# A transformer block on one core: the last key block read in two parts, low parts ahead of reads on GpSimd's queue, normed rows in a tile of their own, and token loads ahead of sums

## The chip, the core and the metric

The kernel runs on one core of a Trainium2 chip. The time is the device time of one execution in microseconds, as a median of several executions. Engines: TensorE (PE, with its weight loads as PEld), VectorE (DVE), ScalarE (ACT), GpSimd (POOL) and SyncE (SP). SP, ACT and POOL issue DMAs, each in the order of its own queue; POOL computes and issues in one and the same order. Engines wait for one another on semaphores.

## The reference

A conditioned transformer block in float32, for x of shape (2, 2048, 576), with 16 heads of 36 and an MLP of 2304:

```
mod = silu(c) @ w_ada + b_ada            # six vectors per batch: shifts, scales, gates
xn  = layernorm(x) * (1 + sc_msa) + sh_msa
q, k, v = split(xn @ w_qkv + b_qkv);  q = layernorm_head(q);  k = layernorm_head(k)
o   = softmax(q k^T / 6) v               # per batch and head
x   = x + g_msa * (o @ w_proj + b_proj)
xn2 = layernorm(x) * (1 + sc_mlp) + sh_mlp
x   = x + g_mlp * (gelu(xn2 @ w1 + b1) @ w2 + b2)
```

## The kernel before

Two bodies are built and one is chosen at run time; for these inputs it is `block_of_small`. Its stages are, for each batch b: inputs (`inputs`), attention (`attend`), output projection (`outputs`); then the MLP for both batches. PE runs in the order in which the program is written throughout. In `inputs`, DVE, SP and POOL run in written order too; in `attend`, DVE, POOL and ACT; in `outputs` and the MLP, DVE alone. The rest is put in order by the scheduler when the program is built.

**Inputs.** 16 token tiles of 128 rows. A tile is loaded (`tile_loaded`), normed, transposed in squares of 32 on DVE, written to DRAM (`squares_turned`, line 1003, four DMAs on POOL) and read back with features on partitions (`turned_loaded`, lines 1011 and 1013, three DMAs). ACT applies scale and shift (line 1020). The last 64 of the 576 features are kept as a rounded high part (line 388) and a low part, which is the difference of an exact copy (`tail`, line 389) and the high part; POOL makes that difference (line 390). A product of a tile (`product`) has, for each half of the columns, eight records of line 1100 and then two of line 1102, of which the second reads the low part. The loop over t calls `begun(t)` (load of tile t+4, read of tile t+2, both on POOL), `modulated_ahead(t)` (ACT's lines and POOL's low part for tile t+1), the products, `turned_ahead(t)` (norm, transposition and writes of tile t+3), and the head norms. In the first batch the first three tiles come another way (transposed on PE), beside the loading and centring of the weights. There `bias_made` centres the bias on DVE and has POOL write it to DRAM, and `bias_spread` has POOL read it back to all partitions.

Q and K are put in DRAM with features as rows (`qk`): `by_feature(t)` transposes on DVE (line 1078) and issues four writes (line 1080), on SP except for the K half of tile 15, which goes on POOL. `take_k_block` reads back the 72 K rows of the first head pair for a range of tiles (lines 812 and 814, four DMAs on SP) and returns a function that applies gain and bias on DVE: line 847 on `km` (32 of 36 features of a head), and lines 847, 856, 857 on `ke` (the remaining four, in high and low parts). The ranges are tiles 0-3, 4-7, 8-11, 12-15. The first three run inside `inputs`; the function of the last is returned as `left`.

**Attention.** For each head pair p (8), query block qb (4 of 512) and key group g (4), one step: `scores` (line 1225: 24 matmul records into eight PSUM banks, then eight exponentials on ACT, line 1229), then `values` of the step before (line 1238: 16 records into one bank), then DVE copies or adds that bank to `ot` (lines 1286, 1288), then the functions due in `later[0]` run. Group g reads columns 256g to 256g+255 of `km` and `ke`, where partitions 0-63 hold keys of tiles 0-7 and partitions 64-127 those of tiles 8-15: group 2 needs tiles 4, 5, 12, 13 and group 3 needs tiles 6, 7, 14, 15. At the first step `left` is put in front of `later[1]`, so it runs at the end of the second step. The gain of the next query block's `qm` is also in `later[1]`, and the three instructions of its `qe` (`parted`) are in `later[2]`.

**Outputs.** Tiles in groups of four. A group's sums are a `whole` part (line 406) and a `halved` part (line 417); the PSUM tile is multiplied by the gate on DVE (line 1362, `evicted`). `summed` then adds the product to the row tile `x1` (line 1374), has POOL write it to DRAM (line 1375) and load a later tile (line 1357). In the first batch the first five tiles of the MLP's input are also made here: after its sum a tile is measured, and at the next call of `summed` it is normed in place (line 1368), transposed and written (`turned`).

**MLP.** Before the first product DVE makes four sums of tokens (`token_sums`, lines 1619 to 1622), and then touches two row tiles with a memset (line 1735), each followed by a load of MLP rows on POOL (line 982). Those tiles are normed and transposed in `ahead`, which DVE reaches before it evicts the first hidden block (`gelu_stored`, lines 1675 to 1683).

Of the kernel before, what the change touches and what calls it, by code (L numbers as in the profile page):

```python
# [31 lines left out]
def dit_block(  # L32
# [719 lines left out]
    def block_of_small():  # L752
# [163 lines left out]
        def first_weights(then):  # L916
# [32 lines left out]
            def bias_made():  # L949
                mean = pool.tile([2 * H, 1], F32, name="mean")  # L950
                nc.vector.tensor_reduce(mean, by_head, AX.X, ALU.add)
                nc.vector.tensor_scalar_mul(mean, mean, 1.0 / HD)
                nc.vector.tensor_scalar(by_head, by_head, mean, None, ALU.subtract)
                saved["bq"] = dram.tile([2 * C], F32, name="bq_kept")
                nc.gpsimd.dma_start(out=saved["bq"].rearrange("(h d) -> h d", d=HD), in_=by_head)

            def bias_spread():
                nc.gpsimd.dma_start(out=bq[:, 0 : 2 * C], in_=saved["bq"].partition_broadcast(P))

            def kept():  # L960
# [82 lines left out]
        def inputs(b, weights, making, work, xnts, turned, loaded):  # L1043

            wq, wq4, bq = weights
            both, squares, taken = {}, {}, []
            key_tiles = (0, 4, 8, 12, 16)

            def squared(t, w0=0, w1=2):
                if squares.get("t") != t:  # L1050
# [20 lines left out]
            def by_feature(t, w0=0, w1=2, ready=True, queue=nc.sync):  # L1071

                begun = [*taken] if ready else []
                if ready:
                    taken.clear()
                part = slice(w0 * C, w1 * C)
                turned_qk = work.tile([P, 2 * C], F32, name="turned_qk", bufs=3)
                nc.vector.transpose(turned_qk[:, part], both[t][:, part])  # L1078
                for g in range(P // SQ):
                    queue.dma_start(  # L1080
                        out=by_square[t, g][:, w0 * NSQ : w1 * NSQ, :],
                        in_=turned_qk[g * SQ : (g + 1) * SQ, part].rearrange("p (k j) -> p k j", j=SQ),
                    )
                for do in begun:
                    do()
                if t == TPB - 1 and w0 == 0:
                    taken.extend(take_q(0, 0))
                if t + 1 in key_tiles and w1 == 2:
                    i = key_tiles.index(t + 1)
                    taken.append(take_k_block(*key_tiles[i - 1 : i + 1]))  # L1090

            def product(w, t, ps=None, steps=(0, 1)):

# [40 lines left out]
            def modulated_ahead(t):  # L1134
                if t + 1 < NT and t + 1 not in modulated:
                    input_modulated(b, xnts[t + 1])
# [3 lines left out]
            if b == 0:  # L1140
                made, ends_made, bias_made, bias_spread, kept = making
                done, modulated = 3, {0, 1, 2}
                ends_made(2)
                rows = {t: tile_normed(loaded.pop(t)) for t in (1, 2)}
                chosen = rows_chosen(work)
                bias_made()
                v = two_steps(2, 0)
                biased(2, v, 0)
                made(0)
                xnts[1] = second_by_feature(rows[1])  # L1150
                v = product(2, 1)
                biased(2, v, 1)
                ends_made(0)
                xnts[2] = second_by_feature(rows[2])
                bias_spread()
                v = product(2, 2)
                biased(2, v, 2)
                gains_by_row(chosen)
                turned_ahead(0)
                made(1)  # L1160
                ends_made(1)
                for t in range(done):
                    q = two_steps(0, t) if t == 0 else product(0, t)
                    biased(0, q, t)

            for t in range(NT - 1):
                begun(t)
                modulated_ahead(t)
                if t >= done:
                    q = product(0, t)  # L1170
                k = product(1, t) if t >= done else two_steps(1, t)
                if t >= done:
                    biased(0, q, t)
                turned_ahead(t)
                if b == 0 and t == 0:
                    turned_ahead(t + 1)
                biased(1, k, t)
                if t > 0:
                    head_scale(t - 1)
# [13 lines left out]
            biased(1, k, t)  # L1193
            squared(t, 1, 2)
            head_scale(t, 1, 2)
            by_feature(t - 1)
            biased(0, q, t)
            squared(t, 0, 1)
            by_feature(t, 1, 2, queue=nc.gpsimd)
            head_scale(t, 0, 1)  # L1200
            biased(2, v, t)
            by_feature(t, 0, 1, ready=False)
# [4 lines left out]
        def attend(b, pool, hooks):  # L1207
# [65 lines left out]
            for p, qb, g in [*steps, (None, None, None)]:  # L1273
# [15 lines left out]
                    if bg == NG - 1:  # L1289
                        later[2 if bp == NPAIR - 1 else 3].append(finish(bp, bqb, ot))  # L1290
                if (p, qb, g) in hooks:
                    later[1] = (hooks[p, qb, g]() or []) + later[1]
                later.append([])
                for do in later.pop(0):
                    do()
# [52 lines left out]
        def outputs(b, weights, between, scratch, turned_of=lambda t: None):  # L1348
# [16 lines left out]
            def summed():  # L1365
                while to_turn:
                    turn, x1, scales = to_turn.pop(0)
                    nc.vector.tensor_scalar(x1, x1, *scales, ALU.subtract, ALU.mult)
                    turn(x1)
                begun = []  # L1370
                while products:
                    t, product = products.pop(0)
# [357 lines left out]
            nc.sync.dma_start(out=hidden[q % len(hidden)], in_=gelus[n][g])  # L1730

        rows_ahead = {}
        token_sums(0)
        for i in (1, 2):
            nc.vector.memset(xs["tiles"][0][0:1, 0:1], 0.0)
            rows_ahead[1, i] = mlp_loaded(1, i, nc.gpsimd)
        for job in range(0, NB * HF, 2):
            (n0, f0), (n1, f1) = divmod(job, HF), divmod(job + 1, HF)
            ahead(job)
# [157 lines left out]
```

## Time and profile before

| what | value |
|---|---|
| runs | 3162.64, 3157.65, 3162.34 us; median 3162.34 |
| the profiled execution | 3161.52 us, of which the span is 3159.7 |
| busy share: PE, DVE, ACT, POOL | 99%, 48%, 47%, 21% |
| PE idle over the span | 3159.7 - 3125.0 = 34.7 us |
| inputs, batch 0 / 1 | 0 to 239.7 / 1096.4 to 1308.2 us |
| attention, batch 0 / 1 | 239.7 to 1021.7 / 1308.2 to 2085.4 us |
| outputs, batch 0 / 1 | 1021.7 to 1096.4 / 2086.2 to 2157.9 us |
| MLP, first / second product | 2158.8 to 2664.3 / 2664.3 us to the end |

A timeline line reads: start, duration, engine and line of the program, operation, what it writes and reads, how many; in brackets the engine's idle time before it and what ended it. A run of like instructions is merged to one line. PE's ends are modelled. A row of the windows gives, for a stretch, each engine's busy time and count, then the TensorE clock that was granted as a share of full speed (PEclk), the share of DMA time and the GB/s moved.

### The profile page before, as it was taken

The numbers are of one execution on the slowest core, as the hardware profiler recorded it, in microseconds if no ns is written. First come the engines' busy times: TensorE is split into PE (matmuls) and PEld (weight loads), VectorE is DVE, ScalarE is ACT, GpSimd is POOL, SyncE is SP. The second block draws the span as 40 slices with busy tenths as digits, with TensorE's granted clock in tenths as the row PEclk, the third lists the DMA queues.
The fourth block names the chain that finished last, engine by engine and source line by source line (L and its number), as shares of the span: only waits on it lengthen the run. The fifth ranks groups of instructions, "written<-read, shape, count | busy, mean of one in ns | idle before, by whom it ended". The sixth has DMA issues, their size and how long they took to land.

```text
span 3159.7 us, 46700 instructions
## 1 busy us (share of the span) xinstructions
PE 3125.0 (99%) x17553; PEld 1860.9 (59%) x17553; DVE 1513.1 (48%) x2173; ACT 1470.5 (47%) x2843; POOL 666.7 (21%) x932
## 2 busy tenths in 40 slices
PE   7999999999999999999999999999999999999999
PEld 5883333333333788633333333358888888777777
DVE  6653443444444556434443444345566554545454
ACT  2326666666666122366666666643555552000000
POOL 4641000011110455200011111012333320112111
PEclk9999999999999999999999999999999999999999
DMA  5753221122221756511122222146545444333331
GB/s 147 175 101 92 78 64 47 55 82 70 64 74 44 234 100 125 86 44 33 46 60 71 78 65 69 56 152 191 165 130 138 131 116 160 110 120 115 117 105 39
DMA packets 300179, 311.94 MB, mean 99 GB/s; under 512 B 178856, under 2 KB 232616, under 8 KB 297832
## 3 DMA queue, kind: packets, MB, share of 16 engines
q1 hardware_dynamic: 251968, 192.19, 21.3%
q0 software_dynamic: 44432, 111.07, 13.5%
q10 hardware_dynamic: 3544, 5.60, 0.5%
q8 instruction: 141, 2.31, 0.3%
q14 instruction: 94, 0.77, 0.1%
HBM read 191.80 MB, written 106.45 MB: 94 GB/s over the span
## 4 chain that ended last, share of the span: by engine, by line
PE 94%; DMA 2%; DVE 1%; issue 1%; SPq 1%; POOL 0%; ACT 0%; DVEq 0%; POOLq 0%; ACTq 0%
PE b L1238 29%; PE b L1225 19%; PE s L1809 15%; PE m L1649 11%; PE s L1100 11%; PE s L406 3%; PE m L1663 2%; PE one L1649 2%; PE s L1102 2%; DMA qk<-turned_qk 0%; DMA xt<-in_x_dram 0%; DMA ke<-qk 0%; PE s L417 0%; DMA xnt<-turned 0%; DVE turned_qk L1078 0%
## 5 line engine op out<-in xcount | busy, mean ns | idle before, releaser
L1229 ACT ACTIVATE pt<-b 128x512 f32<-128x512 f32 x2048 | 1057.7, 608 | 490.5 <-PE b L1238 276.5
L1238 PE MATMUL b<-pt,vt 128*64 128x512 f32 x4096 | 938.1, 600 | 0.0
L1238 PEld LDWEIGHTS b<-pt,vt 128*64 128x64 f32 x4096 | 272.5, 137 | 585.4 <-issue 443.3
L1225 PE MATMUL b<-qm,km 32*128 32x512 f32 x4096 | 570.4, 615 | 3.6 <-DVE km L847 2.3
L1288 DVE TENSOR_TENSOR ot<-b,ot 128x512 f32<-128x512 f32 x192 | 132.8, 692 | 628.5 <-PE b L1238 628.5
L1225 PE MATMUL b<-qe,ke 16*128 16x512 f32 x2048 | 422.8, 791 | 2.1 <-DVE ke L857 2.1
L1100 PE MATMUL s<-wq,xnt 128*128 128x288 f32 x1536 | 403.5, 406 | 2.8 <-ACT xnt L395 2.0
L1225 PEld LDWEIGHTS b<-qm,km 32*128 32x128 f32 x4096 | 191.7, 185 | 278.3 <-ACT pt L1229 211.2
L1809 PE MATMUL s<-ws,as 128*128 128x288 f32 x1440 | 351.8, 406 | 0.0
L1100 PEld LDWEIGHTS s<-wq,xnt 128*128 128x128 f32 x1536 | 280.6, 190 | 65.1 <-ACT xnt L395 1.6
L1809 PEld LDWEIGHTS s<-ws,as 128*128 128x128 f32 x1440 | 273.6, 190 | 75.6
L1257 DVE RECIPROCAL den<-den 128x512 f32<-128x512 f32 x64 | 213.6, 3337 | 10.8 <-DMA den<-den_dram 10.8
L1649 PE MATMUL m<-xnt,wb 128*128 128x256 f32 x864 | 210.3, 379 | 2.0 <-DVE cs L1683 1.1
L1649 PE MATMUL m<-s,wb 128*128 128x256 f32 x864 | 210.0, 379 | 0.0
L1003 POOL DMA_DIRECT2D turned<-squares x212 | 142.5, 678 | 271.5 <-DVE squares L998 262.7
L1649 PEld LDWEIGHTS m<-s,wb 128*128 128x128 f32 x864 | 164.2, 190 | 22.3
L1225 PEld LDWEIGHTS b<-qe,ke 16*128 16x128 f32 x2048 | 107.5, 184 | 117.3 <-issue 112.8
L1286 DVE COPY ot<-b 128x512 f32<-128x512 f32 x64 | 44.3, 692 | 272.6 <-PE b L1238 272.6
L1649 PEld LDWEIGHTS m<-xnt,wb 128*128 128x128 f32 x864 | 158.9, 190 | 21.6 <-issue 1.3
L1687 ACT ACTIVATE cs<-cs,b_sb 128x512 f32<-128x512 f32 x144 | 98.9, 719 | 111.8 <-DVE cs L1682 85.9
L812 POOL DMA_DIRECT2D km<-qk x56 | 28.2, 503 | 577.7 <-PE b L1225 574.9
L1342 POOL DMA_DIRECT2D spare<-in_x_dram x32 | 17.4, 545 | 599.7 <-DVE met L791 599.7
(205 smaller groups left out, 3021.8 us busy)
## 6 DMA issues: line engine op xcount, KB each, us to landing
gelu<-cs SPq DMA_DIRECT2D x144, 256.0 KB
hidden<-gelu SPq DMA_DIRECT2D x16, 2304.0 KB
x_dram<-spare POOLq DMA_DIRECT2D x64, 288.0 KB, 2.5
qk<-turned_qk SPq DMA_DIRECT2D x120, 144.0 KB
qm<-qk SPq DMA_DIRECT2D x256, 64.0 KB
den<-den_dram SPq DMA_DIRECT2D x128, 128.0 KB
turned<-squares POOLq DMA_DIRECT2D x212, 72.0 KB, 2.5
xnt<-turned POOLq DMA_DIRECT2D x54, 256.0 KB, 4.1
```

Of the source, the lines that this page charges most:

```text
L406: nc.tensor.matmul(outs[a], stationary(k, a), moving(k, a), start=(first and k == 0), stop=(not first and k == FULL - 1),)
L1003: queue.dma_start(out=by_square[g], in_=squares[g * SQ : (g + 1) * SQ, :].rearrange("p (k j) -> p k j", j=SQ))
L1100: nc.tensor.matmul(out_a, full[:, k, :], wq[:, k, f], start=k == 0, stop=False)
L1102: nc.tensor.matmul(out_a, parts[:, i, :], wq4[:, f], start=False, stop=i == 1)
L1225: nc.tensor.matmul(ps, k[r, keys], q[r, :], start=first, stop=not first)
L1229: nc.scalar.activation(pt[:, h, :], banks[2 * c + h], AF.Exp, scale=SCALE)
L1238: nc.tensor.matmul(acc[64 * h : 64 * h + 64, :], vt[:, v0 : v0 + 64], pt[:, h, :], start=pt is pts[0][0], stop=pt is pts[-1][0],)
L1257: nc.vector.reciprocal(den, den)
L1288: nc.vector.tensor_tensor(ot, acc, ot, ALU.add)
L1649: nc.tensor.matmul(out_m[m], wb[:, slot[m], k, f * P : (f + 1) * P], moving[m](k), start=k == 0 and m in (1, 2, 5, 6), stop=k == 1 and m == 1,
L1687: nc.scalar.activation(part, part, AF.Gelu, bias=b1_sb[:, g : g + 1])
L1809: nc.tensor.matmul(ms[m], stationary[m][:, f, :], ws[m][:, f, :], start=(f == 0), stop=(f == HF - 1))
```

## The change

Seven edits in five places:

1. In the first batch's inputs the write of the centred bias (POOL) is issued after the low part of tile 1 and not before it (`bias_spread(True)`).
2. In the loop of `inputs`, `modulated_ahead(t)` stands before `begun(t)`: POOL's low part of tile t+1 comes before the load of tile t+4 and the three reads of tile t+2.
3. In the first batch at t = 0 the read of tile 3 (`done` is 3) is issued before the writes of tile 4, and not at t = 1 after them.
4. The last key block is read in two: tiles 12-13 after `by_feature(14)`, tiles 14-15 after the K half of tile 15. Neither is scaled inside `inputs` (`ready=False`).
5. Of the two functions left over, attention runs the first at the end of the second step, as before, and the second one at the end of the third, behind what `later[2]` holds already.
6. In `summed` the normed tile goes to `km[0][:, :576]`, which is idle then, and no longer over `x1`.
7. The two memsets and MLP row loads come before `token_sums(0)`.

```diff
-                nc.gpsimd.dma_start(out=saved["bq"].rearrange("(h d) -> h d", d=HD), in_=by_head)
-
-            def bias_spread():
+
+            def bias_spread(first):
+                if first:
+                    nc.gpsimd.dma_start(out=saved["bq"].rearrange("(h d) -> h d", d=HD), in_=by_head)
+                    return
                 nc.gpsimd.dma_start(out=bq[:, 0 : 2 * C], in_=saved["bq"].partition_broadcast(P))
...
-            key_tiles = (0, 4, 8, 12, 16)
+            key_blocks = {3: (0, 4), 7: (4, 8), 11: (8, 12), NT - 2: (12, 14), NT - 1: (14, NT)}
...
-                if t + 1 in key_tiles and w1 == 2:
-                    i = key_tiles.index(t + 1)
-                    taken.append(take_k_block(*key_tiles[i - 1 : i + 1]))
+                if t in key_blocks and w1 == 2:
+                    taken.append(take_k_block(*key_blocks[t]))
...
                 xnts[1] = second_by_feature(rows[1])
+                bias_spread(True)
...
                 xnts[2] = second_by_feature(rows[2])
-                bias_spread()
+                bias_spread(False)
...
             for t in range(NT - 1):
+                modulated_ahead(t)
                 begun(t)
-                modulated_ahead(t)
...
+                if b == 0 and t == 0:
+                    xnts[done] = input_loaded(turned.pop(done), nc.gpsimd)
+                    turned_ahead(t + 1)
                 turned_ahead(t)
-                if b == 0 and t == 0:
-                    turned_ahead(t + 1)
...
-            by_feature(t - 1)
+            by_feature(t - 1, ready=False)
             biased(0, q, t)
             squared(t, 0, 1)
-            by_feature(t, 1, 2, queue=nc.gpsimd)
+            by_feature(t, 1, 2, ready=False, queue=nc.gpsimd)
...
                 if (p, qb, g) in hooks:
-                    later[1] = (hooks[p, qb, g]() or []) + later[1]
+                    due = hooks[p, qb, g]() or []
+                    later[1] = due[:1] + later[1]
+                    later[2] = due[1:] + later[2]
...
                     turn, x1, scales = to_turn.pop(0)
-                    nc.vector.tensor_scalar(x1, x1, *scales, ALU.subtract, ALU.mult)
-                    turn(x1)
+                    normed = km[0][:, :C]
+                    nc.vector.tensor_scalar(normed, x1, *scales, ALU.subtract, ALU.mult)
+                    turn(normed)
...
         rows_ahead = {}
-        token_sums(0)
         for i in (1, 2):
             nc.vector.memset(xs["tiles"][0][0:1, 0:1], 0.0)
             rows_ahead[1, i] = mlp_loaded(1, i, nc.gpsimd)
+        token_sums(0)
```

## The prediction

> **What bounds the kernel now.** I read the page's busy shares and chain first, then who PE waited for, then the timeline of every engine around each such wait.
>
> ```profile
> PE 3125.0 (99%) x17553; PEld 1860.9 (59%) x17553; DVE 1513.1 (48%) x2173; ACT 1470.5 (47%) x2843; POOL 666.7 (21%) x932
> ...
> PE 94%; DMA 2%; DVE 1%; issue 1%; SPq 1%; POOL 0%; ACT 0%; DVEq 0%; POOLq 0%; ACTq 0%
> ```
>
> PE is busy for 3125.0 of 3159.7 us and holds 94% of the chain. No edit removes a matmul, so only PE's idle time, 34.7 us, and any slowing of its clock can move the end. PE's waits, total and count:
>
> ```profile
> PE s L1102 <- POOL xnt L390: 3.0, 2, 1.5
> PE b L1225 <- DVE km L847: 2.3, 1, 2.3
> PE b L1225 <- DVE ke L857: 2.1, 2, 1.4
> ...
> PE s L406 <- DVE product L1362: 1.5, 1, 1.5
> PE m L1649 <- DVE cs L1683: 1.1, 1, 1.1
> PE s L417 <- DVE product L1362: 1.0, 1, 1.0
> ```
>
> About 10 us more is the wait for the first rows, which no edit touches. Every line shown lies where the diff works. At attention's start PE also spreads out; the start for batch 1:
>
> ```profile
> 1319.96 1.13 PE L1225 MATMUL b<-qm,km 32*128 32x512 f32 x4
> 1323.41 0.79 PE L1225 MATMUL b<-qm,km 32*128 32x512 f32 x2 [2.32 <-DVE km L847]
> ...
> 1325.37 0.79 PE L1225 MATMUL b<-qe,ke 16*128 16x512 f32 x2 [0.75 <-DVE ke L857]
> ...
> 1328.23 5.55 PE L1238 MATMUL b<-pt,vt 128*64 128x512 f32 x16
> ```
>
> A quiet step has 24 score records in 2.39 us and 16 value records in 3.59 (262.62 to 265.01 to 268.60). Here the third scores take 8.27 and the next values 5.48. In batch 0 it is 6.65 and 4.81. The values are late because the clock falls (rows of PEclk, three columns from the end):
>
> ```profile
> 254.00:258.00 4.00, 2.64 (x19) 1.06 (x18) 2.30 (x4) 1.08 (x2) 0.11 (x1) 0.86 0.71 139
> 258.00:260.00 2.00, 2.00 (x6) 0.58 (x6) 0.00 (x0) 0.09 (x1) 0.00 (x0) 0.50 1.00 382
> ...
> 1324.00:1328.00 4.00, 3.25 (x20) 1.51 (x14) 1.79 (x4) 1.08 (x2) 0.11 (x1) 0.66 0.41 96
> ```
>
> Work lost in batch 0: 4x0.14 + 2x0.5 + 3x0.05 (260-263 shows 0.95) = 1.7 us; in batch 1: 4x0.34 + 3x0.5 + 3x0.18 (1331-1334 shows 0.82) = 3.4 us. Both follow PE gaps: 1.02 + 1.36 us and 2.32 + 0.75. After the single gaps of 1.5 us in the inputs the clock stayed at 1.00.
>
> **The change, part by part.**
>
> *Bias write behind the low part.* Tile 1's tail ends at 28.77, but POOL issues the bias write at 29.54 (0.52 us) and only then, at 30.07, makes the low part; PE goes on at 30.59. Without the DMA in front: 28.77 + 0.07 + 0.47 + 0.05 = 29.36. Gain 1.2 us. The moved write still waits for DVE's centring (29.24), so it leaves at 29.5 as before; its reader is at 36.46.
>
> *Low part ahead of the reads; tile 3 read early.* The tail of tile 3 ends at 67.45; POOL is issuing a load and three reads from 66.62 to 69.06, the low part follows at 69.08, and PE loses 1.45 at 69.60. In the new order it is done by 68.0, when PE asks for it (68.15). Gain 1.45. The reads (2.4 us of issue) now stand behind a low part that waits for ACT. In later tiles the tail is done about when PE frees the buffer (95.62 against 95.66), so they slip by some 0.5 us, and PE shows no wait in either batch's remaining tiles: nothing. Tile 3's read (1.9 us of issue, three DMAs) now waits for PE's k of tile 0, about 57.2, in front of the four writes of tile 4 (57.75) and the load of tile 5 (60.39), which slip by up to 1.9 us; their reader starts at 64.38 on DVE and no PE wait hangs on it. Zero, with 0 to 0.5 us in the range.
>
> *Normed rows beside their tile.* DVE's norm in place must wait until the write of the same rows to DRAM has landed:
>
> ```profile
> 1060.01 0.58 DVE L1368 TENSOR_SCALAR spare<-spare,mv,rstd 128x576 f32<-128x576 f32 x1 [7.81 <-DMA x_dram<-spare]
> ...
> 1075.03 0.58 DVE L1368 TENSOR_SCALAR spare<-spare,mv,rstd 128x576 f32<-128x576 f32 x1 [6.81 <-DMA x_dram<-spare]
> ...
> 1077.65 1.42 DVE L1362 TENSOR_TENSOR product<-s,gate 128x576 f32<-128x576 f32 x2
> ```
>
> The waits are 7.81, 0.84 and 6.81 us. The eviction at 1077.65 frees the bank for which PE waits 1.47 until 1078.46. With a tile of its own the norm at 1075.03 follows the evictions of 1066.82 at about 1068.2, and the eviction falls well ahead of 1076.99, where PE asks. Gain 1.47. The other PE wait, 1.03 at 1067.61, has another end: DVE's reciprocal at 1066.74 waits for ACT, which stands from 1050.7 to 1065.26 at a read queued behind the weights. It stays unless ACT's order changes: 0 to 1.03, I take 0.
>
> *Loads ahead of token sums.* DVE's memsets come at 2162.48, after four sums of 2.5 us; POOL loads at 2162.85, data 5.6 us later. POOL is writing rows until 2160.84, so the loads go 2.0 us sooner. PE's wait behind that chain is 1.07 at 2174.06; the sums move by 0.1 us and their first use is at 2161.43. Gain 1.07.
>
> *The last key block in two.* DVE's rows at batch 0's start:
>
> ```profile
> 251.30 0.69 DVE L1286 COPY ot<-b 128x512 f32<-128x512 f32 x1 [2.81 <-PE b L1238]
> 252.65 0.55 DVE L847 TENSOR_SCALAR km<-km,gb_at 64x512 f32<-64x512 f32 x1 [0.66 <-DMA km<-qk]
> ...
> 255.07 0.75 DVE L857 SCALAR_TENSOR_TENSOR ke<-ended,part,high 64x512 fp32r<-64x512 f32 x1
> ...
> 262.76 0.69 DVE L1288 TENSOR_TENSOR ot<-b,ot 128x512 f32<-128x512 f32 x1 [6.36 <-PE b L1238]
> 263.37 0.54 DVE L847 TENSOR_SCALAR ended<-qe,gb_at 128x512 f32<-128x512 f32 x1
> ...
> 264.47 0.75 DVE L857 SCALAR_TENSOR_TENSOR qe<-ended,part,high 128x512 fp32r<-128x512 f32 x1
> ```
>
> Now the data are late (km at 252.65 waits 0.66, ended 0.76 for its read). New: rows 12-13 are asked for after tile 14's writes, at about 242 instead of 247.6, and land before DVE is free of the copy to `ot`. A 64x512 instruction takes 0.55, 0.55, 0.48, 0.75. For 64x256 the nearest pair is the MLP's adds, 0.42 for 128x256 against 0.69: factor 0.6, so 0.33 for km and about 1.05 for the other three. From 251.91 DVE has km at 252.24 and ke at 253.3. PE needed 1.98 after ke (255.83 to 257.81), part of it slowed; about 1.65 at full clock. So the third scores end at 254.95, 3.8 us after 251.16: lost 1.4.
>
> But the second half stands in `later[2]`, and the fourth scores need it. After the second values (end V) DVE adds to `ot` (V+0.14 to V+0.75), makes `qe` (three instructions, 1.8 us by 263.37 to 265.2), and only then the second half: km at V+2.95, ke at V+4.0. PE starts the fourth scores at V and can finish them at V+5.6, against V+2.4: lost 3.2, where before nothing was. Per attention 4.6 is lost by waits, against 3.8 and 4.4 before (6.65 + 4.81 - 5.98 - 1.7; 8.27 + 5.48 - 5.98 - 3.4). The waits therefore grow, by 1.1 in all, and what decides is the clock: 5.1 us lost before, and unknown after. The new gap in the fourth scores is 1.84 us by modelled ends (V+1.13 to V+2.97), between the 1.5 that left the clock and the 2.4 in two pieces that cost 1.7. Nearest is the first, but not by much; I take one such loss for the two attentions, 1.7. Bounds: 0 and 6.8 (3.4 each). Gain 5.1 - 1.1 - 1.7 = 2.3, between 4.0 and -2.8. Four more DMAs per attention on SP (0.3 to 0.6 us each) pass in front of the query reads and tile 15's Q writes, which SP otherwise spends waiting for the K writes (to 247.54).
>
> The Trainium skill, "TensorE: Matmul & The Clock Gate", section "HAM oscillation", gives the rule that gaps up to some 3.4 us do no harm. The rows above show 0.50 after shorter gaps, so the measurement decides; by the page nothing would be lost after the change and the sum would be 9.2.
>
> **Sum.** 1.2 + 1.45 + 1.47 + 1.07 + 2.3 = 7.5 us. The profiled execution took 3161.5 (span 3159.7 plus 1.8 around it); the median is 0.8 above it. 3162.3 - 7.5 = 3154.8.
>
> **Rivals.**
>
> *A: the clock falls in every new gap (same).* For: gaps of 2.4 and 3.1 us did it. Against: the new one is a single 1.84. At 3.4 per attention: 5.2 (the other four edits) + 5.1 - 1.1 - 6.8 = 2.4, 3159.9; at 1.7 each, 5.8, 3156.5.
>
> *B: all covers hold (faster).* The clock stays up (+1.7) and ACT is no longer parked, so the 1.03 goes too: 10.2, 3152.1. For: 1.5 us did no harm; DVE is sooner at its measuring.
>
> *C: the split costs twice (slower).* Rows 12-13 are issued behind the query reads of the next block, which in batch 1 hold SP until 1315.8; they then land by about 1323.4, as ke's read did (6.01 us). Third and fourth scores both open a gap and the clock falls after each: 1.7 after the third, 3.4 after the fourth, in both attentions, 10.2 in place of 1.7, and 1.0 of wait. 7.5 - 8.5 - 1.0 = -2.0: 3164.3. It decides once the clock's losses and that wait pass 9.2 us together. Against it: DVE is held by the copy to `ot` until 251.9 and 1320.7 anyway, so late reads cost little.
>
> *D: the order of the unordered queues moves elsewhere.* SP, ACT and POOL are reordered by the scheduler in `outputs`; if POOL is parked at tile 1's low part (idle 9.78 to 1066.22 now) ahead of eight writes (5.31 us) and two row loads, the gain of 1.47 turns to a loss of some 2.5 (half of the writes' 5.31): 7.5 - 1.5 - 2.5 = 3.5, 3158.8.
>
> **Numbers.** Forecast 35%, A 27%, B 20%, C 8%, D 10%. 0.2% is 6.3 us, about what a measurement of this kernel can tell from no change: faster means below 3156.0. The forecast stands 1.2 us inside, and the runs of before spread over 5.0; of forecast and B some 46 points fall there, of A and D 7. Slower, above 3168.7, needs more than C: 6. Same: 41. The forecast's own range is 3153 to 3157; B and C's side open it to 3150 to 3162.5.
>
> **What would show it.** PE's waits for POOL's low part gone or at 0.3; no DVE wait at line 1368; PE's 1.07 at line 1649 gone. In attention the third scores 3.8 us long, the fourth 5.6, with `qe`'s three rows between the add and the second km. Wrong if the fourth scores are quiet, if the clock is below 1.00 for more than 10 us, or if PE waits anew for a low part in `inputs`.

## The result and the profile after

The changed kernel takes 3149.52 us (median of 7 runs, 3149.18 to 3153.96), the kernel before 3162.64 beside it (7 runs, 3157.65 to 3164.58). The ratio is 0.9963, 95% interval 0.9951 to 0.9975: 13.1 us or 0.4% faster, where the prediction's sum had 7.5, and just below the low end of its range, 3150.

Shares and PE's busy time, from the page of the changed kernel:

```profile
PE 3125.2 (99%) x17553; PEld 1862.0 (59%) x17553; DVE 1515.6 (48%) x2181; ACT 1471.2 (47%) x2843; POOL 664.2 (21%) x932
```

PE is idle for 25.0 us of the span's 3150.2 (before: 34.7). Who it waited for, total, times and longest:

```profile
PE s L1103 <- POOL xnt L390: 1.1, 2, 0.8
PE b L1228 <- issue: 1.0, 4, 0.3
...
PE m L1655 <- DVE cs L1689: 0.5, 1, 0.5
```

The low part's 3.0 us are down to 1.1, the MLP's 1.07 to 0.55, and the two waits in `outputs` are gone. Of attention's waits (2.3 and 2.1 us in all) four gaps of some 0.25 us are left. The start of attention for batch 1, PE's timeline:

```profile
1314.93 1.13 PE L1228 MATMUL b<-qm,km 32*128 32x512 f32 x4
...
1319.02 3.65 PE L1241 MATMUL b<-pt,vt 128*64 128x512 f32 x16
1322.60 1.13 PE L1228 MATMUL b<-qm,km 32*128 32x512 f32 x4
1323.96 0.79 PE L1228 MATMUL b<-qm,km 32*128 32x512 f32 x2 [0.23 <-issue]
...
1326.68 3.65 PE L1241 MATMUL b<-pt,vt 128*64 128x512 f32 x16
```

Third and fourth scores take 4.09 and 4.08 us (before: 8.27 and 2.4), the values behind them 3.58 and 3.59 (before: 5.48 behind the third scores). Each of these steps still loses 1.7 us to a quiet one (a step in which PE waits for nothing, 2.39 us), in batch 0 as well. The windows of the same stretch, the granted clock third from the end:

```profile
1314.00:1318.00 4.00, 3.77 (x22) 1.32 (x22) 2.28 (x5) 1.94 (x5) 0.00 (x0) 1.00 0.91 174
...
1322.00:1326.00 4.00, 3.77 (x28) 1.48 (x24) 3.11 (x7) 1.94 (x5) 0.00 (x0) 1.00 0.59 147
```

The clock stays at 1.00 here and in batch 0's attention too. Why the fourth scores lose no more than the third is seen on DVE:

```profile
1322.72 0.69 DVE L1291 TENSOR_TENSOR ot<-b,ot 128x512 f32<-128x512 f32 x1 [2.76 <-PE b L1241]
1323.44 0.42 DVE L847 TENSOR_SCALAR km<-km,gb_at 64x256 f32<-64x256 f32 x1
1323.77 0.42 DVE L847 TENSOR_SCALAR ended<-ke,gb_at 64x256 f32<-64x256 f32 x1
...
1324.62 0.48 DVE L857 SCALAR_TENSOR_TENSOR ke<-ended,part,high 64x256 fp32r<-64x256 f32 x1
1325.14 0.55 DVE L847 TENSOR_SCALAR ended<-qe,gb_at 128x512 f32<-128x512 f32 x1
```

The second half of the key block (`km` at 1323.44, `ke` done at 1325.10) runs *in front of* the three instructions of `qe`. The diff says so: `later[2] = due[1:] + later[2]`. The text ahead of the result has it wrong, twice: item 5 of the change ("behind what `later[2]` holds already") and the prediction's "makes `qe` ..., and only then the second half". Both are a misreading of the diff.

In `outputs` of batch 0 DVE's norm goes to `km` without a wait; one wait appears at the transposition and is hidden:

```profile
1048.94 0.57 DVE L1374 TENSOR_SCALAR km<-spare,mv,rstd 128x576 f32<-128x576 f32 x1
...
1054.47 0.78 DVE L1000 STREAM_TRANSPOSE spare<-km 128x576 f32<-128x576 f32 x1 [3.43 <-DMA turned<-spare]
```

PE has no wait left in that stage, so the 1.03 is gone as well as the 1.47. The reason is ACT's order, after and then before:

```profile
1057.63 0.29 ACT L276 ACTIVATE std<-mv,eps 128x1 f32<-128x1 f32 x1 [10.12 <-DVE mv L274]
1065.46 0.49 ACT L388 ACTIVATE xnt<-xnt,mod 128x128 fp32r<-128x128 f32 x1 [7.54 <-DMA xnt<-turned]
```

```profile
1065.26 0.49 ACT L388 ACTIVATE xnt<-xnt,mod 128x128 fp32r<-128x128 f32 x1 [14.57 <-DMA xnt<-turned]
...
1066.42 0.28 ACT L276 ACTIVATE std<-mv,eps 128x1 f32<-128x1 f32 x1
```

The standard deviation of the next tile (1057.63) now stands ahead of the scale and shift that waits for its read until 1065.46. Before, it stood behind that same kind of instruction (1066.42 behind 1065.26), and the product's eviction waited behind it.

Stage by stage, from the boundaries of PE's work in the two profiled executions (before minus after):

| stage | gain, us |
|---|---|
| up to PE's first product of the inputs | -2.5 |
| inputs, batch 0, the rest | 1.8 |
| attention, batch 0 / 1 | 2.0 / 4.4 |
| outputs, batch 0 | 3.2 |
| inputs, batch 1, and the step into attention | 0.5 |
| MLP | 0.1 |
| sum | 9.5 = 3159.7 - 3150.2 |

The first row belongs to that execution, not to the change: PE's first product came at 22.1 us, and most executions of the kernels below, which share that start, have it at 19.1 to 19.7 (before: 19.5; one has 22.3). Those 2.5 us are also what the profiled execution, 3152.0, stands above the median.

### The profile page after: what moved, and what is told of

It is laid out like the page before. It is cut to its first block, busy times and chain, and to the rows that moved or that the text cites. A ratio compares the mean times of both kernels' runs of the same rounds, so it can differ in the third digit from the quotient of the medians.

```text
span 3150.2 us, 46743 instructions
## 1 busy us (share of the span) xinstructions
PE 3125.2 (99%) x17553; PEld 1862.0 (59%) x17553; DVE 1515.6 (48%) x2181; ACT 1471.2 (47%) x2843; POOL 664.2 (21%) x932
## 5 line engine op out<-in xcount | busy, mean ns | idle before, releaser
L1655 PEld LDWEIGHTS m<-s,wb 128*128 128x128 f32 x864 | 164.2, 190 | 22.3
L1022 ACT ACTIVATE xnt<-xnt,mod 128x128 f32<-128x128 f32 x244 | 100.4, 481 | 102.1 <-DMA xnt<-turned 94.6
```

The lines of the kernel that those rows point to most:

```text
L1022: nc.scalar.activation(part, part, AF.Identity, **affine(which, k, b))
L1655: nc.tensor.matmul(out_m[m], wb[:, slot[m], k, f * P : (f + 1) * P], moving[m](k), start=k == 0 and m in (1, 2, 5, 6), stop=k == 1 and m == 1,
```

## The experiments

All are edits of the changed kernel, timed beside the kernel before, which took 3162.1 to 3163.2 us there. "Lost" is a stage's time over that of the same stage with quiet steps: attention, from its first values to its last, takes 768.67 us in batch 0 and 761.23 in batch 1 when no step is stretched (the kernels with the sooner halves, less their stretches). By that measure the kernel before lost 5.5 + 7.8 us and the changed one 3.4 + 3.4.

### The key block: whole, behind `qe`, sooner

```diff
 whole:
-            key_blocks = {3: (0, 4), 7: (4, 8), 11: (8, 12), NT - 2: (12, 14), NT - 1: (14, NT)}
+            key_blocks = {3: (0, 4), 7: (4, 8), 11: (8, 12), NT - 1: (12, NT)}
-            by_feature(t - 1, ready=False)
+            by_feature(t - 1)
-            by_feature(t, 1, 2, ready=False, queue=nc.gpsimd)
+            by_feature(t, 1, 2, queue=nc.gpsimd)
-                    later[1] = due[:1] + later[1]
-                    later[2] = due[1:] + later[2]
+                    later[1] = due + later[1]
 second half behind qe:
-                    later[2] = due[1:] + later[2]
+                    later[2] = later[2] + due[1:]
 both halves a step sooner:
-                    later[1] = due[:1] + later[1]
-                    later[2] = due[1:] + later[2]
+                    later[0] = due[:1] + later[0]
+                    later[1] = due[1:] + later[1]
```

> The changed kernel with the last key block read and made in one piece again (edits 4 and 5 undone), all else kept. Theory 1 (the split gains by itself, in both attentions): third scores and the values after them back at 6.65 + 4.81 us in batch 0 and 8.3 + 5.5 us in batch 1, the granted clock down to 0.5 to 0.9 behind them, and 6.4 us longer than the changed kernel (2.06 + 4.39 by the two profiles). Rival (the gain in batch 1 comes from the other edits, which move the reads before it): only some 2 to 4 us longer, with the clock at 1.00 in one of the two batches.

> The changed kernel with one thing turned: the second half of the key block stands behind the three instructions of qe in later[2] and not in front of them, the order that the prediction assumed. Theory 1 (only the wait grows, the clock stays up): fourth scores 5.6 to 6.0 us instead of 4.1 in both batches, 3.0 to 3.8 us longer in all, clock 1.00. Rival (the prediction's case A, the clock falls in a gap of that length): the same waits, and 1.7 to 3.4 us of work lost after each of them, 6.4 to 10.6 us longer in all, with the clock at 0.5 to 0.9 for 3 to 7 us.

> The changed kernel with each half of the last key block made one step sooner: the first half in later[0], before the copy of the first values, the second in later[1], before the addition of the second values. Theory 1 (the 1.7 us that third and fourth scores each still lose is only DVE's place in the order, the rows have landed by then): third and fourth scores 2.4 to 2.6 us in both batches, 6 to 7 us shorter than the changed kernel, some 3143. Rival (the rows land late: in batch 1 the reads of tiles 14 and 15 are issued until 1313.1, those of the query until later): the third scores gain 1.7 and the fourth nothing, 3 to 3.5 us shorter; or DVE waits ahead of the copy and the values behind it wait for their bank: nothing gained.

| kernel | median, range (runs), us | lost in attention, batch 0 + 1 | of it the clock |
|---|---|---|---|
| before | 3162.64 | 5.5 + 7.8 | 1.7 + 3.4 |
| changed | 3149.52 | 3.4 + 3.4 | 0 + 0 |
| whole block again | 3155.8, 3153.6 to 3157.8 (11) | 6.7 + 6.3 | 3.4 + 3.4 |
| second half behind `qe` | 3155.8, 3152.8 to 3158.9 (11) | 9.7 + 6.8 | 5.1 + 1.7 |
| both halves sooner | 3143.37, 3141.8 to 3144.0 (5) | 1.4 + 0 | 0 + 0 |

The clock's share is the sum of (1 - granted clock) over windows of 1 us. The last two columns are one profiled execution each.

*Whole:* 6.3 us longer in the medians, 6.2 in the two attentions of the profile: the split carries the gain in attention by itself, in both batches.

*Behind `qe`:* this is the kernel that the prediction's working describes. DVE and PE in batch 0:

```profile
256.75 0.69 DVE L1291 TENSOR_TENSOR ot<-b,ot 128x512 f32<-128x512 f32 x1 [1.48 <-PE b L1241]
257.36 0.54 DVE L847 TENSOR_SCALAR ended<-qe,gb_at 128x512 f32<-128x512 f32 x1
...
259.24 0.42 DVE L847 TENSOR_SCALAR km<-km,gb_at 64x256 f32<-64x256 f32 x1
...
260.41 0.48 DVE L857 SCALAR_TENSOR_TENSOR ke<-ended,part,high 64x256 fp32r<-64x256 f32 x1
```

```profile
259.76 1.31 PE L1228 MATMUL b<-qm,km 32*128 32x512 f32 x2 [2.02 <-issue]
...
264.41 6.25 PE L1241 MATMUL b<-pt,vt 128*64 128x512 f32 x16
```

From the addition to the second half's `km` it is 2.49 us where it was 0.72 above, PE's gap in the fourth scores is 2.02, the values behind take 6.2, and the clock falls in both batches. Of the 6.3 us in the medians some 3.5 are the longer waits (1.76 each), so about 2.8 are the clock; in the profiled execution the clock's part is larger. The order of two list operands is worth as much as the split itself.

*Sooner:* 6.15 us shorter than the changed kernel, 0.9939 of the kernel before (0.9926 to 0.9953). It beats both. DVE in batch 1:

```profile
1309.20 0.42 DVE L847 TENSOR_SCALAR km<-km,gb_at 64x256 f32<-64x256 f32 x1 [2.63 <-DMA km<-qk]
...
1310.89 0.69 DVE L1289 COPY ot<-b 128x512 f32<-128x512 f32 x1
1311.62 0.42 DVE L847 TENSOR_SCALAR km<-km,gb_at 64x256 f32<-64x256 f32 x1
```

The rows had landed by 1309.2; in the changed kernel DVE made nothing of them before 1315.78, since they stood behind the copy of the first values. So in this execution the 1.7 us of each step in batch 1 were DVE's order and not the data. That does not hold in every execution: in the four other profiles below in which the first half is made sooner, DVE gets `km`'s rows at most 0.7 us ahead of the third scores of batch 1 (1.3 here), and these are stretched by 1.0 to 1.7 us. In batch 0 DVE waits 3.03 us for `km`'s rows and PE still loses 1.4 in the third scores; the landing moves by about 1 us from one execution to the next (below).

### The norm in place again

```diff
-                    normed = km[0][:, :C]
-                    nc.vector.tensor_scalar(normed, x1, *scales, ALU.subtract, ALU.mult)
-                    turn(normed)
+                    nc.vector.tensor_scalar(x1, x1, *scales, ALU.subtract, ALU.mult)
+                    turn(x1)
```

> The changed kernel with the norm in place again (edit 6 undone). Theory 1 (edit 6 also changed ACT's order, since the scheduler places ACT's instructions by it): both PE waits in the first batch's outputs come back, 1.47 and 1.03, and the stage is 74.5 to 74.8 us instead of 71.5: 3.0 to 3.2 us longer. Rival (ACT's order comes from another edit): only the wait of 1.47 comes back, the stage is 73.0 us.

3153.28 us (3152.6 to 3155.2, 9 runs): 3.8 longer. The stage takes 76.1 us in place of 71.5. The waits on DVE, then on PE, then the windows behind PE's wait:

```profile
1060.06 0.16 DVE L278 RECIPROCAL rstd<-std 128x1 f32<-128x1 f32 x1 [1.11 <-ACT std L276]
...
1069.60 0.58 DVE L1373 TENSOR_SCALAR spare<-spare,mv,rstd 128x576 f32<-128x576 f32 x1 [8.06 <-DMA x_dram<-spare]
```

```profile
1073.02 9.72 PE L406 MATMUL s<-wp,qo 128*128 128x288 f32 x32 [2.61 <-DVE product L1367]
```

```profile
1074.00:1076.00 2.00, 2.00 (x6) 1.40 (x5) 2.00 (x4) 1.36 (x4) 2.00 (x4) 0.51 0.75 164
1076.00:1078.00 2.00, 2.00 (x7) 1.42 (x6) 1.63 (x3) 0.00 (x0) 1.50 (x4) 0.64 0.83 182
```

Theory 1 is right that edit 6 also moves ACT's order: DVE's reciprocal waits again for a deviation that stands behind ACT's parked instruction (1.11 us). But the order isn't that of before either. The two PE waits, 1.03 and 1.47, have become one of 2.61, and behind it the clock falls, 1.7 us of work, which they had not caused: 2.61 + 1.7 of the stage's 4.6.

### The inputs and the MLP's first loads

```diff
 bias write and reads back:
+                bias_spread(True)
                 xnts[1] = second_by_feature(rows[1])
-                bias_spread(True)
...
-                modulated_ahead(t)
                 begun(t)
+                modulated_ahead(t)
 tile 3's read and the loads back:
-                if b == 0 and t == 0:
-                    xnts[done] = input_loaded(turned.pop(done), nc.gpsimd)
-                    turned_ahead(t + 1)
                 turned_ahead(t)
+                if b == 0 and t == 0:
+                    turned_ahead(t + 1)
...
+        token_sums(0)
         for i in (1, 2):
             nc.vector.memset(xs["tiles"][0][0:1, 0:1], 0.0)
             rows_ahead[1, i] = mlp_loaded(1, i, nc.gpsimd)
-        token_sums(0)
```

> The changed kernel with edits 1 and 2 undone: the bias write in front of tile 1's low part, and the load and the reads in front of the low part in the loop; edit 3 (tile 3 read early) stays. Theory 1 (each wait comes from POOL's issues in front of the low part): PE waits 1.5 us again at tile 1's low part, some 30 us into the run, and the wait of 0.84 at the next low part is gone, since PE gets there later; at tile 3's low part 1.2 to 1.5 us. In sum 1.5 to 2.5 us longer. Rival (edit 3 alone mends tile 3, its read being early): no wait at tile 3, 0.3 to 0.8 us longer.

> The changed kernel with edits 3 and 7 undone: tile 3 read behind the writes of tile 4, and the MLP's first row loads behind the token sums. Theory 1 (for tile 3 edit 2 is what counts, and the row loads are held by the weights' transfers): no or at most 0.3 us of wait at tile 3; at the MLP's start PE's wait behind the first hidden block goes from 0.5 to 1.0 or 1.1. In sum 0.5 to 0.9 us longer. Rival (edit 3 carries the gain at tile 3): PE waits 1.0 us or more at tile 3, 1.5 to 2.1 us longer.

With the bias write and the reads back, 3151.28 us (3149.95 to 3152.21, 5 runs), 1.8 longer. PE:

```profile
30.55 0.40 PE L1103 MATMUL s<-wq,xnt 128*128 128x288 f32 x1 [1.50 <-POOL xnt L390]
...
69.52 0.40 PE L1103 MATMUL s<-wq,xnt 128*128 128x288 f32 x1 [1.42 <-POOL xnt L390]
```

Both waits are back (1.50 and 1.42), and the new one of 0.84 at the third low part is gone, as theory 1 had it. With tile 3's read and the loads back, 3150.23 us (3149.62 to 3153.08, 5 runs), 0.7 longer: PE shows no wait at tile 3, its products there are stretched by 0.3, and the MLP's wait is 1.1 again. So at tile 3 the low part's place counts and the early read hardly does. Undone in these four pieces, the edits are worth 6.3 (key block), 3.8 (norm), 1.8 and 0.7 us, 12.6 of the 13.1 measured.

Two more edits were tried on top of the sooner halves, to explain the 0.84 and the MLP's remainder: (a) DVE centres the second half of the Q weights after their last rows; (b) a DVE memset holds the loads of the second weights back.

```diff
 (a)
-                made(0)
+                made(0, (0,))
                 xnts[1] = second_by_feature(rows[1])
...
-                biased(2, v, 1)
                 ends_made(0)
+                biased(2, v, 1)
+                made(0, (1,))
 (b)
+            nc.vector.memset(ws[m][0:1, 0, 0:1], 0.0)
             quarter = w2[k * HF * P : (k + 1) * HF * P, n * HALF : (n + 1) * HALF]
```

> The version with both halves of the last key block a step sooner, and two more edits. (a) In the first batch's inputs DVE centres the second half of the Q weights behind their last rows, so that no large DVE product of two tiles runs beside POOL's low part of tile 2. Theory 1 (DVE's operation of 1.36 us beside it is what stretches POOL's low part from 0.46 to 1.36 us): 0.45 to 0.6 us for it, and PE's wait of 0.84 gone; rival (something else, such as the transfers): 1.3 us again and the wait stays. (b) In the MLP the loads of the second weights wait for DVE to pass the first jobs. Theory 1 (they fill the DMA queues ahead of the first row loads): the rows land 5 us or less after their issue in place of 7.2, and PE's wait of 0.6 us is gone; rival (the rows' landing hangs on the write before it): still 6 us or more. By theory 1 in both, 1.2 to 1.5 us less than with the sooner halves alone, some 3142.0.

> Both halves of the last key block a step sooner, and the second half of the Q weights centred behind their last rows, without the edit on the second weights' loads. Expected if the stages add: the inputs of the first batch 0.75 us shorter than with the sooner halves alone, the rest the same, some 3142.6. Rival: the landing of rows 12 and 13 differs by about 1 us from one execution to the next and hides it: 3143 to 3144.

The second of these is (a) alone. The changed kernel's POOL, its DVE product at that time, and POOL with (a):

```profile
37.56 1.36 POOL L390 TENSOR_TENSOR xnt<-tail,xnt 128x128 fp32r<-128x128 f32 x1 [4.68 <-ACT tail L389]
```

```profile
37.25 1.36 DVE L905 TENSOR_TENSOR wq<-wq,sums 128x1152 f32<-128x1152 f32 x1
```

```profile
34.85 0.61 POOL L390 TENSOR_TENSOR xnt<-tail,xnt 128x128 fp32r<-128x128 f32 x1 [4.68 <-ACT tail L389]
```

In the changed kernel POOL's instruction begins at 37.56 and ends at 38.92, DVE's began before it and ends at 38.61. With (a) DVE's product of that size comes later; the low part takes 0.61 and PE's wait is gone: the inputs are 0.75 shorter. The Trainium skill, "SBUF — State Buffer", section "SBUF: two separate sides", says that a DVE operation with two inputs in SBUF and a POOL operation that reads SBUF share a port pair, and that whichever starts first holds it until it ends, while the other waits. The 1.36 against 0.46 agrees.

For the MLP's loads, DVE's first measuring of the loaded rows in the changed kernel, then with (b):

```profile
2158.59 0.82 DVE L272 BATCH_NORM_STATS2 st<-xt 128x6 f32<-128x288 f32 x2 [5.45 <-DMA xt<-x_dram]
```

```profile
2147.17 0.82 DVE L272 BATCH_NORM_STATS2 st<-xt 128x6 f32<-128x288 f32 x2 [2.39 <-DMA xt<-x_dram]
```

With the weights held back DVE waits 2.39 us for the rows in place of 5.45. That the rows were late because of the weights' transfers is shown. But PE then waits 0.6 us in a later job, behind the new memset, and the MLP takes as long as before.

Neither is a gain in the end: 3143.37 (3142.2 to 3144.8, 4 runs) with both and 3143.81 (3142.6 to 3145.9, 5 runs) with (a) alone, against 3143.37. In the profiled executions the 0.75 is there, and in both the third scores of batch 1 are stretched by 1.1 to 1.7 us, where they were quiet with the sooner halves alone: rows 12 and 13 landed later in relation to PE. (a) isn't needed for that: the two kernels of the next section with the first half sooner and without (a) show 1.0 and 1.6 us in the same place.

### What makes the clock fall

What the prediction left open decides 0 to 7 us here. Idle work on DVE (a scratch tile of 128x512 made again) sets the length of PE's gap in the fourth scores:

```diff
+                    again = [lambda: nc.vector.tensor_scalar(high, ended, sign_q, None, ALU.mult)]
-                    later[2] = due[1:] + later[2]
+                    later[2] = (again * (2 + b) if due else []) + due[1:] + later[2]
 one gap, and shorter gaps, besides:
-                    later[1] = due[:1] + later[1]
+                    later[0] = due[:1] + later[0]
 shorter gaps: again * (1 + b)
```

> The changed kernel with idle work on DVE (a scratch tile of 128x512 made again, some 0.5 us each) in front of the second half of the last key block: two of them in batch 0, three in batch 1. PE's gap in the fourth scores then is some 1.2 us in batch 0 and 1.7 us in batch 1, between the 0.25 us of the changed kernel, after which the clock stayed up, and the 2.0 us of the order with qe in front, after which it fell in both batches. If the length of the gap decides (a limit between 1.5 and 2.0 us): clock 1.00 in batch 0, open in batch 1, where a fall puts the limit between 1.2 and 1.7; waits of 1.0 and 1.5 us in all, 2.5 us longer, and 1.7 to 5 us more if the clock falls. If what decides is what went before (two waits close together, the third and the fourth scores): the clock falls in both, 6 to 12 us longer.

> As the kernel with the longer gaps, with the same idle work in front of the second half (two operations in batch 0, three in batch 1), but with the first half made a step sooner, so that the third scores hardly wait and the gap in the fourth scores (1.2 us in batch 0, 1.7 us in batch 1) stands alone. If the gap's length decides: the clock falls again as with the longer gaps, and the third scores' 3.4 us are all that is gained, some 3151. If what went before decides (third scores stretched by 1.7 us, then the gap): the clock stays at 1.00 in both batches, some 3148 to 3149 (fourth scores 5.1 and 5.6 us against 4.1 in the changed kernel, third scores 2.4 to 3.0).

> The kernel with the longer gaps once more, for a second profile. If the clock's fall depends on the program alone, it falls again after both gaps, for about as long. If it depends on more than the program (the runs of this kernel spread from 3149.9 to 3156.8 us), it falls after one of them only, after none, or for another length of time.

Longer gaps: 3154.62 us, from 3149.9 to 3156.8 in 8 runs, and 3153.3 once more. One gap: 3153.04, from 3148.4 to 3155.7 in 6 runs. The clock fell in both batches of all three profiles: a single gap of 1.17 us is enough, so neither the length that I had supposed (1.5 to 2.0) nor the step before decides. That gap in batch 0 of the kernel with one gap, then the windows in front of the fall and behind it:

```profile
257.29 1.17 PE L1228 MATMUL b<-qm,km 32*128 32x512 f32 x2 [1.17 <-issue]
```

```profile
250.73:254.15 3.42, 3.42 (x26) 1.15 (x20) 0.55 (x1) 2.35 (x6) 0.11 (x1) 1.00 0.49 114
254.15:257.56 3.41, 2.24 (x14) 0.63 (x12) 2.33 (x6) 1.51 (x4) 0.00 (x0) 1.00 0.93 262
257.56:260.97 3.41, 3.41 (x20) 2.15 (x18) 2.62 (x5) 1.08 (x2) 0.00 (x0) 0.50 0.85 332
```

Nor does the program alone decide: in the kernel with longer gaps batch 1 lost 3.4 us in one execution and 1.7 in the other.

The edges of the low clock say more, read in windows of 0.1 us. In the kernel before they lie at 256.90, 260.31, 1325.27 and 1332.09: 1, 313.00 and 315.00 times 3.4133 us behind the first. The five other executions above with a fall in both attentions have the same grid, each with its own start, to 0.004 of a step. So the loss comes in portions of 3.413/2 = 1.707 us, and a fall begins at a tick of this grid, not at the wait itself. PE's busy share in the stretch that ended where the clock fell, by its records:

| execution, batch | PE's gap, us | busy share | low for | lost |
|---|---|---|---|---|
| before, 0 / 1 | 1.02+1.36 / 2.32+0.75 | 0.60 / 0.36 | 3.4 / 6.8 | 1.7 / 3.4 |
| whole block, 0 / 1 | 1.27+0.71 / 1.32+0.49 | 0.45 / 0.61 | 6.8 / 6.8 | 3.4 / 3.4 |
| behind `qe`, 0 / 1 | 2.02 / 2.00 | 0.50 / 0.64 | 10.2 / 3.4 | 5.1 / 1.7 |
| longer gaps, 0 / 1 | 1.17 / 1.67 | 0.66 / 0.51 | 3.4 / 6.8 | 1.7 / 3.4 |
| longer gaps again, 0 / 1 | 1.18 / 1.67 | 0.66 / 0.51 | 3.4 / 3.4 | 1.7 / 1.7 |
| one gap, 0 / 1 | 1.17 / 1.67 | 0.66 / 0.51 | 3.4 / 10.2 | 1.7 / 5.1 |

In attention no stretch at full clock with 0.70 or more was followed by a fall. In the inputs and outputs, whose stationary operands have mostly 128 rows and not 32 or 16, stretches with 0.56 to 0.59 were followed by none and one with 0.30 (the norm in place) was. In between the share doesn't decide: a stretch with 0.53 at the first products of batch 0 was followed by a fall of one step in four profiles, the changed kernel's among them, and by none in two (the one with the second half behind `qe` and the one with both (a) and (b)). In the changed kernel:

```profile
19.64:23.05 3.41, 1.80 (x11) 1.17 (x8) 2.12 (x12) 1.59 (x5) 1.38 (x5) 1.00 1.04 307
23.05:26.46 3.41, 3.41 (x8) 2.36 (x8) 2.27 (x6) 1.13 (x4) 0.98 (x2) 0.50 1.08 361
```

It cost little: from the first product to the second tile's, the profile with (a) alone takes 7.43 us with such a fall, and the one with (a) and (b) 7.26 without it, since there PE waits 0.79 us for weights instead. The rule for attention came from these profiles, so one more kernel tested it:

> As the kernel with the single gap, with one idle operation less in each batch: one in batch 0, two in batch 1, so the gaps are some 0.7 and 1.2 us. Theory (formed from the profiles before this one): the clock is set anew at ticks 3.413 us apart, on one grid through the whole execution, and it is halved for the next stretch where PE was busy for less than some 0.66 to 0.70 of the stretch just ended, by the records, in attention. Then a gap of 1.2 us halves it only where most of it lies in one stretch (1.2 / 3.413 leaves 0.65, the 0.7 of batch 0 leaves 0.79): no fall in batch 0, in batch 1 a fall where the gap is not cut by a tick, none where it is; each fall lasts a whole number of 3.413 us and costs 1.707 of work, and its edges lie on one grid with any other of the same execution. Rival (each gap above some length halves the clock by itself): batch 1 falls in every execution, so the runs differ by 1 us at most. By the theory they lie at some 3147 where nothing falls and 1.7 or 3.4 us above it where it does.

Its windows, cut at the ticks of its own grid:

```profile
257.97:261.38 3.41, 2.76 (x22) 1.28 (x20) 3.20 (x8) 1.09 (x2) 0.00 (x0) 1.00 1.02 378
...
1321.39:1324.80 3.41, 2.26 (x22) 1.30 (x20) 3.20 (x8) 0.81 (x2) 0.00 (x0) 1.00 0.77 173
1324.80:1328.21 3.41, 3.41 (x14) 0.77 (x8) 0.82 (x2) 0.61 (x2) 0.00 (x0) 0.50 0.22 66
1328.21:1331.62 3.41, 3.41 (x24) 1.18 (x24) 0.69 (x1) 2.82 (x6) 0.00 (x0) 1.00 0.18 53
```

The gap of 0.65 us in batch 0 left 0.81 and no fall; that of 1.15 in batch 1 lay whole in one stretch, left 0.66, and the clock fell at its end for one step. That is what the rule said. But it doesn't rule out the rival, a limit on the gap's length. The runs are 3147.4, 3148.4, 3148.9 and 3153.2: not within 1 us of each other, as the rival had it, but 3153.2 lies at none of the theory's places either (some 3147, and 1.7 or 3.4 above). It is the profiled run, with a single fall. In this profile the third scores of each batch are stretched by 1.6 us, in batch 1 behind rows that came late, and the MLP is 1.0 us longer than in most:

```profile
1313.06 0.42 DVE L847 TENSOR_SCALAR km<-km,gb_at 64x256 f32<-64x256 f32 x1 [4.55 <-DMA km<-qk]
```

So the runs' spread can't be put down to the clock alone. A limit on length between 1.02 us (kernel before, batch 0, its first gap: share 0.70, no fall) and 1.15 would fit attention's profiles as well, with the fall put off to the next tick; a longer gap that a tick cuts into two stretches of 0.70 or more would tell, and none came. What is shown is the grid and the portions; what the clock weighs, and what keeps it low for one, two or three steps, stays open.

## Why the prediction was right and wrong

The sign and the places were right: every wait that the prediction named is gone or smaller, at no place was a new one over 1 us put on PE, and 3149.5 is 5.3 below the forecast. That the misreading did the sign no harm is luck: the order that stands in the program is kinder than the one that was costed. Of its three signs of being wrong one came, a new wait of PE for a low part in `inputs` (0.84). Point by point, by its own terms:

- *Bias write behind the low part, 1.2.* Measured 1.23 (1.50 to 0.27). But PE now gets to the third low part sooner, where POOL stands behind DVE's 1.36 us product: 0.84 given back. "What is late next" wasn't asked.
- *Low part ahead of the reads, 1.45.* Measured 1.45. The early read of tile 3, which the prediction put beside it, is worth 0.3.
- *Normed rows, 1.47.* Measured 3.2 with the 1.03 and 0.7 more that no PE wait shows. The term's upper bound named ACT's order as what would free the 1.03; it did. With that, case B had this stage right.
- *Loads ahead of sums, 1.07.* Mis-sized: the wait fell by 0.52. The loads were issued 2.0 us sooner and landed 0.5 sooner, since the second weights' loads leave in the same moment; the step "5.6 us later" took the landing time as fixed, and it grew to 7.1. In the whole MLP 0.1 is left.
- *The key block, 2.3.* Measured 6.4. The step that failed is "the second half stands in `later[2]`" behind `qe`: it stands in front. That puts the fourth scores at 4.1 us and not 5.6, and the gap at 0.25 and not 1.84. 1.4 and 3.2 of wait were forecast, 1.7 and 1.7 came; 1.7 of clock was forecast, none came. The third scores' 3.8 was 4.1: the three instructions behind `km` take 1.33 us, in the third scores as in the fourth (1323.77 to 1325.10), where 1.05 had been scaled down from 64x512. Half the columns left 0.72 of the durations (1.67 of 2.33), not 0.6.

The forecast of 3154.8 lies 1.0 from the 3155.8 of the kernel that it described without knowing. That isn't the working being right: there the clock fell in both batches, as case A said at its lower price (3156.5), while `outputs` gave 1.7 more than either had. "Nearest is the first, but not by much", the choice between no fall and one, was wrong for that kernel: its single gaps of 2.0 us were no safer than the two before.

Cases C and D did not come about: SP's reads of rows 12 and 13 left right behind tile 14's writes (242.7), ahead of the query's, and PE had no wait for a reordered queue. The four added reads on SP, put at 0.3 to 0.6 us of issue each, took 0.4 to 2.4, and no wait of PE shows for it.

On the clock the Trainium skill, "TensorE: Matmul & The Clock Gate", has two statements. In "What's actually happening" it says that the clock is set by a free-running window of 3413 ns; the grid above agrees, over a thousand microseconds of one execution. The rule that the prediction weighed ("HAM oscillation", gaps up to some 3.4 us do no harm) doesn't hold in attention here: 1.15 us did.

## What to carry to other kernels

Where work is queued in lists, write the lists out, element by element, before costing the order: one `a + b` read as `b + a` moved 6 us here. A wait of PE cost its length here, and where the clock fell at the next tick also 1.7 us or a multiple, so a gap cut to a few tenths can gain more than its length; look for it in the granted clock behind the wait, not in the waits alone. When a wait is gone, ask what the engine runs into sooner, and before asking for data earlier, whether DVE's own order is what leaves landed rows lying: the two halves of a key block made a step sooner gave another 6.15 us, 3143.4 in all.

## What the runs showed of the hardware

- The clock's edges lie on one grid of 3.413 us through each execution, and losses come in portions of 1.707 us. Kernels with such falls spread more from run to run (3152.8 to 3158.9 with the second half behind `qe`) than the one with sooner halves and none in attention (3141.8 to 3144.0). The changed kernel, with none there either, has five runs within 0.5 us and two at 3152.0 and 3154.0. That the ticks' place makes the spread isn't shown, since only profiled executions show the clock, and late rows move a run as well.
- A busy share of 0.66 between two ticks was followed by a fall in attention; 0.56 wasn't in stages with mostly 128 rows of stationary operand, and 0.53 there was in four executions of six. That the rows count is an inference; stages with other row counts weren't tried.
- POOL's subtraction of 128x128 takes 0.46 us and 1.36 beside a DVE product of 128x1152.
